# One PSUM bank for the filter layer, two for the sums, and sums last in a step, in a graph layer on one core

## The chip, the cores and the metric

The kernel runs on one core of a Trainium2 chip. The engines of the core are TensorE (PE, with its weight loads PEld), VectorE (DVE), ScalarE (ACT), GpSimd (POOL) and SyncE (SP, which issues most of the DMAs). PSUM, the memory that TensorE writes into, has eight banks of 512 f32 numbers a partition. The metric is the time of one execution in microseconds (us), the median of repeated runs.

## The reference

One layer of message passing on a graph of 12500 atoms and 412500 edges, each atom and each filter with 128 features. Each edge goes from a `src` row to a `dst` row; `dst` is sorted, `src` is not. Cut to what is computed:

```python
h = jnp.maximum(_layernorm(x), 0.0)
h = h @ W_in2f                                   # 12500 x 128
Wij = ssp(edge_attr_20 @ W_f1 + b_f1) @ W_f2 + b_f2   # filter layer, 412500 x 128
Wij = Wij * edge_weight[:, None]
x_ij = h[dst] * Wij                              # a message for each edge
agg = segment_sum(x_ij, src, 12500)              # summed by src
out = x + ssp(agg @ W_o1 + b_o1) @ W_o2 + b_o2
```

`ssp` is softplus less log 2.

## The kernel before, in words

The edges are cut into 828 **chunks** of up to 512 edges, four chunks to a **group**. For each chunk the kernel computes the hidden layer of the filter from 20 edge features (`hidden`, L819: TensorE matmuls into a tile `z`), softplus of it in two steps on ScalarE (`hidden_exp`, L828, with a running sum into `exps` that is checked at the end, and `hidden_log`, L835), the filter values (`value`, L935: four 128-column products into a bank `v`, onto a bias that ScalarE wrote there at L932), the rows of h that belong to the edges (`pick`, L944, into a bank `picked`; `picked`, L952, scales them on ScalarE into `hg`) and the message `o` = v times hg (`message`, L961, VectorE at L968 or L1107). Each message row is then written to a **slot** in a table in HBM that belongs to its source row's block of 128 atoms. `put` (L971) does that with GpSimd: one indirect DMA for each 128 rows, so four for a chunk (L977). The slot numbers come from ranks that TensorE counts in the bank `free` (`rank`, L847: matmuls at L900 and L867) and VectorE reads (`rank_end`, L871: L872).

32 of the groups (the list `SORTED`) are **permuted**: their chunks hold 424 edges and are sorted by source block on the chip beforehand, so that three quarters of the rows go to fixed places with plain DMAs and only one indirect DMA a chunk is left (L1113). `Permute` prepares such a group some 19 steps ahead; `move` (L1295) multiplies by one-hot matrices, into the same tile `z` as the filter layer, and `moved` (L1303) copies the result out on ScalarE.

The edges are also cut into seven segments, each with its own table. When a segment's table is full, `Collect` reads it back in units: `load` (a DMA into a tile `m`, five buffers), `compare` (VectorE, L1388: a one-hot matrix `to`), `add` (TensorE, L1404: the products are summed in a bank `acc`, four blocks to a bank) and `keep` (VectorE, L1427, or ScalarE, L1425, for the first segment: the bank is added to `agg`). The last segment is collected behind the last chunk, together with the output layer (`finish`, L555), which writes `out`.

The order of the work on each engine is written out by hand in `step(k)` (L1487), called once for each chunk: each engine executes its instructions in the order in which `step` names them, and waits on semaphores where it needs another's result. The step works on several chunks at once: in step k the message of chunk k, the value of k+1, the pick of k+2, the rank of k+6 and the hidden layer of k+4. A scatter of chunk k also waits until pick k+2 is done (`PACE`, L26), and a scatter that writes into one of the 16 views of a table waits for the one before it in that view.

The eight banks of before: `z` has two (both chunks of a pair), `acc` one, `v` three in turn (shared by `picked`), `free` one, and `bank` one, half of it constants and half of it room for counts. The layer norm's `xps` and `hps` (L476, L484) use the `acc` bank as well.

Of the kernel before, what the change touches and what calls it, by code (L numbers as in the profile page):

```python
# [18 lines left out]
P = 128  # L19
# [48 lines left out]
def gnn_kernel(  # L68
# [151 lines left out]
    exps = sbuf("exps", [P, ceil_div(NCH, 2)])  # L220
# [93 lines left out]
    def ranges(psum):  # L314
# [13 lines left out]
        nbad = psum.tile([P, QT, P], F32, name="nbad", tag="acc")[:1, 0, :1]  # L328
# [103 lines left out]
    def late_biases(psum):  # L432

        nc.vector.tensor_scalar(nbo1, bo1, -1.0, None, op0=ALU.mult)
        b12 = psum.tile([P, QT, P], F32, name="b12_out", tag="acc")[:, 0, :]
        nc.tensor.matmul(b12, bo1.to_broadcast([P, P]), wo2, start=True, stop=True)
        nc.vector.tensor_add(bo2, b12, bo2)
# [5 lines left out]
    def make_h(q, psum, halves=False):  # L443
# [32 lines left out]
        xps = psum.tile([P, QT, P], F32, name="xps", tag="acc")  # L476
# [7 lines left out]
        hps = psum.tile([P, QT, P], F32, name="hps", tag="acc")  # L484
# [69 lines left out]

    def finish(t0, n, sT, quad, psum, z, xo=None, bank=("v", 3)):  # L555
# [26 lines left out]
    def anyway(edge, quad, psum):  # L582
# [10 lines left out]
        with tc.For_i(0, NGA, 1) as g:  # L593
# [15 lines left out]
            for c in range(NCHUNK):  # L609
                z = psum.tile([P, 2, CH], F32, name="z")[:, 0, :]  # L610
# [43 lines left out]
        for t0 in range(0, NTILE, QT):  # L654
# [8 lines left out]
            z = psum.tile([P, 2, CH], F32, name="z_out", tag="z")[:, 0, :]  # L663
# [4 lines left out]
    with tc.tile_pool(name="edge", bufs=2) as edge, tc.tile_pool(  # L668
        name="quad", bufs=3
    ) as quad, tc.tile_pool(name="psum", bufs=1, space=PSUM) as psum, tc.tile_pool(name="state_ps", bufs=1, space=PSUM) as state_ps:  # L670
        NB = 2
# [61 lines left out]
        class Group:  # L733


            def __init__(self, g):
# [31 lines left out]
                self.out = {}  # L768

# [49 lines left out]
            def hidden(self, c):  # L819

                z = psum.tile([P, 2, CH], F32, name="z")
                for k in range(2):
                    rows = slice(32 * (c + k), 32 * (c + k) + RBF)
                    nc.tensor.matmul(z[:, k, :], wf1[rows, :], self.f[rows, :],  # L824
                                     start=True, stop=True)
                self.pair[c] = z

            def hidden_exp(self, c):  # L828
                z = self.pair[c]
                i = (self.g * NCHUNK + c) // 2  # L830
                r = quad.tile([P, 2, CH], F32, name="r", bufs=RB)
                nc.scalar.activation(r, z, AF.Exp, bias=bf1, accum_out=exps[:, i:i + 1])  # L832
                self.pair[c] = r

            def hidden_log(self, c):  # L835
                r = self.pair[c]
# [162 lines left out]
        class Permuted(Group):  # L999
# [22 lines left out]
            def hidden(self, c):  # L1022

                z = psum.tile([P, 2, CH], F32, name="z")
                ev = self.from_.ev[c // 2]
                for k in range(2):
                    for q in range(3):
                        nc.tensor.matmul(z[:, k, :], w1s[:, q, :], ev[:3 * WR, k, :],
                                         start=q == 0, stop=q == 2)
                self.pair[c] = z  # L1030
# [95 lines left out]
        class Permute:  # L1126


            def __init__(self, g):
# [30 lines left out]
            def bank(self):  # L1160
                if not self.early:
                    return room_ps
                t = psum.tile([P, QT, P], F32, name="acc_p", tag="acc")
                return t.rearrange("p c f -> p (c f)")

            def load(self):
                if self.early:
                    a0 = rows_at + 5 * NC + 8 + self.w0 // NCHUNK % 2 * (256 + 2 * QB)
                    assert a0 + 256 + 2 * QB <= NTILE * P
# [125 lines left out]
            def move(self, c):  # L1295
                if c % 2 == 0:
                    self.z = psum.tile([P, 2, CH], F32, name="z")
                parts = self.slabs.pop(c).bitcast(BF16).rearrange("p (j n h) -> p j n h", j=QT, h=2)
                for j, h in enumerate(self.hot.pop(c)):
                    nc.tensor.matmul(self.z[:, c % 2, :], parts[:, j, :, 1], h, start=j == 0,  # L1300
                                     stop=j == QT - 1)

            def moved(self, c):  # L1303
                self.ev[c // 2] = quad_room().bitcast(BF16).rearrange("p (w e) -> p w e", w=2)
                nc.scalar.activation(self.ev[c // 2], self.z, AF.Copy)
# [31 lines left out]
        class Collect:  # L1337


            def __init__(self, seg):  # L1340
# [15 lines left out]
                self.banks = [("acc", 1)]  # L1356
# [36 lines left out]
            def add(self, u):  # L1393
                b0, nb, t0, nt = self.units[u]
                m, to = self.m.pop(u), self.to.pop(u)
                for j in range(nb * nt):
                    b, t = b0 + j // nt, t0 + j % nt
                    i = b % self.size
                    if i == 0 and t == 0:
                        tag, bufs = self.banks[b // QT % len(self.banks)]  # L1400
                        self.acc[b // QT] = psum.tile([P, QT, P], F32, name="acc", tag=tag,
# [497 lines left out]
```

## Time and profile before

| what | us |
|---|---|
| median of three runs | 3897.16 (3892.02 to 3898.47) |
| the profiled execution, its own time | 3887.55 |
| its span, first to last instruction | 3885.5 |
| TensorE busy | 3319.8 |
| VectorE busy | 3054.3 |
| GpSimd busy | 2829.7 |
| ScalarE busy | 2477.1 |

The rows quoted below have these columns. In a group of instructions: line, engine, operation, `out<-in` with partitions x elements and type, xcount, then busy time in all, mean ns of one, and the idle time of the engine just before them with what ended most of it. In a row of the timeline: start, duration, engine, line, operation, count, and in brackets the idle time before it and what released it. "issue" is idle time in which the engine waited for nothing that the profile shows. In a table of stretches: busy time of each engine with its number of instructions, the granted clock of TensorE, the share of the DMA engines' time and what they moved. DMAs that SyncE issues stand as SPq.

### The profile page before, as it was taken

The page shows a single profiled execution, that of the slowest core. Times are in us where ns is not written, and L with a number is a line of the kernel's source. Part 1 is how long each engine was busy: PE and PEld are TensorE (multiplying, and loading weights), DVE is VectorE, ACT ScalarE, POOL GpSimd, SP SyncE. Part 2 cuts the span into 40 slices and gives each one's busy share as a digit, 9 for nine tenths or more (in the row PEclk, how much of TensorE's full clock was granted, in tenths as well). Part 3 has the DMA queues.
Part 4 walks back from the last instruction along what each step waited for, and adds up shares of the span by engine and source line. Part 5 has one row for each costly group of instructions (what it writes and reads, how often), then busy time and mean ns, then how long its engine had stood idle before and what let it go on. Part 6 is the DMA issues. An engine that isn't in the chain of part 4 may idle for free. (4 is left out here: it accounts for less than half of the span.)

```text
span 3885.5 us, 79865 instructions
## 1 busy us (share of the span) xinstructions
PE 3319.8 (85%) x24510; PEld 2644.5 (68%) x24560; DVE 3054.3 (79%) x8306; ACT 2477.1 (64%) x5728; POOL 2829.7 (73%) x2946
## 2 busy tenths in 40 slices
PE   6787887877778888888889989998989989898869
PEld 4555555545457677677667777777778777787767
DVE  7887878776668778887788878888877777788777
ACT  5777777867667766676667666666555555565525
POOL 5777777777777777777777777777777777777760
PEclk9888888888789999999999999999999999999999
DMA  6787767755567776688767788788988898777767
GB/s 172 220 281 246 198 185 193 201 172 149 155 197 224 214 214 191 184 245 248 197 185 198 210 260 241 217 225 264 282 232 228 227 271 237 224 226 209 194 195 192
DMA packets 669996, 835.54 MB, mean 215 GB/s; under 512 B 238252, under 2 KB 475700, under 8 KB 669560
## 3 DMA queue, kind: packets, MB, share of 16 engines
q1 hardware_dynamic: 575432, 636.64, 59.9%
q0 software_dynamic: 93696, 193.58, 15.0%
q8 instruction: 198, 3.24, 0.4%
q14 instruction: 238, 1.95, 0.2%
q10 hardware_dynamic: 432, 0.13, 0.0%
HBM read 425.40 MB, written 404.54 MB: 214 GB/s over the span
## 5 line engine op out<-in xcount | busy, mean ns | idle before, releaser
L977 POOL DMA_INDIRECT slots<-o,slot x2800 | 2702.6, 965 | 898.9 <-issue 610.9
L1404 PEld LDWEIGHTS acc<-to,m 128*128 128x128 f32 x8328 | 1056.9, 204 | 342.3 <-DVE to L1388 130.7
L1404 PE MATMUL acc<-to,m 128*128 128x128 f32 x8328 | 1142.7, 293 | 149.0 <-DVE to L1388 63.1
L939 PEld LDWEIGHTS v<-wf,r 128*128 128x128 f32 x6624 | 924.3, 208 | 140.1 <-ACT v L932 79.8
L939 PE MATMUL v<-wf,r 128*128 128x128 f32 x6624 | 960.6, 292 | 53.1 <-ACT v L932 52.9
L832 ACT ACTIVATE r<-z,bf 128x1024 f32<-128x1024 f32 x414 | 459.7, 1110 | 662.6 <-PE z L824 587.6
L957 ACT ACTIVATE hg<-picked,rcut 128x128 f32<-128x128 f32 x2800 | 791.6, 369 | 77.9 <-PE picked L948 72.3
L932 ACT ACTIVATE v<-bf 128x512 f32<-128x512 f32 x826 | 497.0, 602 | 427.7 <-DVE o L968 365.4
L1388 DVE TENSOR_TENSOR to<-count_ps,m 128x640 f32<-128x640 f16 (+4 forms) x939 | 666.2, 736 | 55.3 <-DMA m<-slots 29.0
L968 DVE TENSOR_TENSOR o<-v,hg 128x512 f32<-128x512 f32 x700 | 478.7, 684 | 108.5 <-ACT hg L957 57.0
L837 ACT ACTIVATE r<-r,half 128x1024 f32<-128x1024 f32 x414 | 470.4, 1136 | 0.0
L872 DVE TENSOR_REDUCE top<-free 128x4 f32<-128x392 f32 x700 | 388.3, 555 | 93.4 <-PE free L867 92.1
L948 PE MATMUL picked<-near,at 96*128 96x128 bf16 x2800 | 289.2, 228 | 189.7 <-DVE o L968 83.3
L824 PE MATMUL z<-f,wf 20*128 20x512 f32 x1400 | 431.2, 694 | 0.0
L841 DVE TENSOR_TENSOR inb<-count_ps,blk 128x392 f16<-128x392 f16 x700 | 388.5, 556 | 51.8 <-PE count_ps L1239 39.7
L948 PEld LDWEIGHTS <-at 96*128 96x128 bf16 x2800 | 230.0, 103 | 224.5 <-issue 193.5
L900 PE MATMUL free<-inb,rest_of 128*128 128x392 f16 x732 | 258.5, 353 | 49.1 <-DVE top L872 48.5
L966 DVE COPY o<-place 128x8 f32<-128x8 f32 x350 | 68.3, 195 | 241.4 <-DMA slots<-o,slot 195.6
L867 PE MATMUL free<-inb,after 128*128 128x392 f16 x700 | 248.3, 355 | 8.5 <-DVE used L906 6.0
L919 DVE TENSOR_SCALAR at<-rel,prow 96x512 bf16<-96x512 bf16 x700 | 252.9, 362 | 0.0
L1113 POOL DMA_INDIRECT slots<-o,slot_p x128 | 124.4, 972 | 39.0 <-issue 18.0
L1097 ACT ACTIVATE hg<-picked,scalars 128x128 f32<-128x128 f32 x512 | 144.3, 366 | 4.1 <-PE picked L1085 3.9
(228 smaller groups left out, 2735.1 us busy)
## 6 DMA issues: line engine op xcount, KB each, us to landing
m<-slots SPq DMA_DIRECT2D x458, 322.5 KB
rel<-rel_d SPq DMA_DIRECT2D x175, 384.0 KB
m<-slots SPq DMA_DIRECT2D x150, 387.0 KB
slots<-zero SPq DMA_DIRECT2D x106, 516.0 KB
slots<-o,slot POOLq DMA_INDIRECT x2800
f<-in_f_n SPq DMA_DIRECT2D x412, 80.0 KB
slots<-zero SPq DMA_DIRECT2D x122, 258.0 KB
fix<-o SPq DMA_DIRECT2D x128, 193.5 KB
```

The source lines that it names most:

```text
L824: nc.tensor.matmul(z[:, k, :], wf1[rows, :], self.f[rows, :], start=True, stop=True)
L832: nc.scalar.activation(r, z, AF.Exp, bias=bf1, accum_out=exps[:, i:i + 1])
L837: nc.scalar.activation(r, r, AF.Ln, bias=half, scale=0.5)
L841: nc.vector.tensor_tensor(inb, count_ps[:, None, :NBLK].to_broadcast([P, QT, NBLK]), self.blk[:, c * QT:(c + 1) * QT, None].to_broadcast([ ...
L932: nc.scalar.activation(v, spread(bf2, QT), AF.Copy)
L939: done = nc.tensor.matmul(v[:, i, :], r[:, i * P:(i + 1) * P], wf2, start=False, stop=True, skip_group_check=True)
L948: done = nc.tensor.matmul(ps[:, i, :], at[:, i * P:(i + 1) * P], near, start=i == 0, stop=i == QT - 1, skip_group_check=True)
L957: nc.scalar.activation(hg[:, i, :], ps[:, i, :], AF.Copy, scale=self.rcut[:, j:j + 1])
L968: nc.vector.tensor_mul(o[:, :, :P], v, hg)
L977: put = nc.gpsimd.indirect_dma_start(out=views[j % VIEWS], out_offset=bass.IndirectOffsetOnAxis(ap=self.slot[:, j:j + 1], axis=0), in_=o[: ...
L1388: nc.vector.tensor_tensor(to[:p, a:e, :], count_ps[:p, None, :].to_broadcast([p, e - a, P]), self.m[u][:p, a:e, P:].to_broadcast([p, e - a ...
L1404: nc.tensor.matmul(self.acc[b // self.size][:, i, :], m[:p, j, :P], to[:p, j, :], start=t == 0, stop=t == self.seg.read(b) - 1)
```

## The change

The banks are dealt out anew. `z` has one bank, and the filter layer's first product and its exponential go chunk by chunk instead of by pairs; the logarithm still takes a pair. The freed bank becomes a second one for sums: `acc_quad` hands out `acc0` and `acc1` in turn, and while a sum is open, the other one to everybody else. The moves of the sorting take these banks, one chunk at a time, instead of `z`. `exps` has a column for each chunk. The output layer's two `z_out` are `z` and `acc1`, no longer the halves of `z`. The order inside a step changes: the window (L919) comes first, the logarithm and then the exponential stand behind the message and the scatters, ranks come ahead of the hidden layer, which runs five chunks ahead instead of four, and the layer norm's second half, `keep` and `add` come last.

```diff
+    turns = {"last": 1, "held": None, "pool": None}
+    def acc_quad(name):
+        t = 1 - (turns["last"] if turns["held"] is None else turns["held"])
+        turns["last"] = t
+        return turns["pool"].tile([P, QT, P], F32, name=name, tag=f"acc{t}")
...
             def hidden(self, c):
-                z = psum.tile([P, 2, CH], F32, name="z")
-                for k in range(2):
-                    rows = slice(32 * (c + k), 32 * (c + k) + RBF)
-                    nc.tensor.matmul(z[:, k, :], wf1[rows, :], self.f[rows, :],
-                                     start=True, stop=True)
-                self.pair[c] = z
+                z = psum.tile([P, CH], F32, name="z")
+                rows = slice(32 * c, 32 * c + RBF)
+                nc.tensor.matmul(z, wf1[rows, :], self.f[rows, :], start=True, stop=True)
+                self.z_of[c] = z
...
                 nc.scalar.activation(r, z, AF.Exp, bias=bf1, accum_out=exps[:, i:i + 1])
...
             def move(self, c):
-                if c % 2 == 0:
-                    self.z = psum.tile([P, 2, CH], F32, name="z")
+                self.z = acc_bank("z_p")
...
-                    put(-9 + c // 2 * 2, "product", self.move, c)
-                for c in range(0, NCHUNK, 2):
-                    put(-8 + c, "moved", self.moved, c)
+                    put(-10 + c, "product", self.move, c)
+                    put(-9 + c, "moved", self.moved, c)
...
-                        self.acc[b // QT] = psum.tile([P, QT, P], F32, name="acc", tag=tag,
-                                                      bufs=bufs)
+                            home = acc_quad("acc")
+                            turns["held"] = turns["last"]
...
-        LG, LW, LR, LZ = 10, 6, 6, 4
+        LG, LW, LR, LZ = 10, 6, 6, 5
...
             statics.clear()
+            part("window", k + 3, window)
             sorting(k, "moved")
-            part("log", min(k + LZ - 2, made["exp"]), pairs(hidden_log))
-            part("exp", min(k + LZ - 1, made["hidden"]), pairs(hidden_exp))
...
+            part("log", min(k + LZ - 2, made["exp"] - (made["exp"] < NCH - 1)), pairs(hidden_log))
...
+            for c, u in units:
+                c.compare(u)
+                compared.append((c, u))
             if has(k):
                 g, c = of(k)
                 g.put(c)
-            part("window", k + 3, window)
-            for c, u in units:
-                c.compare(u)
-                compared.append((c, u))
-            for c in owed:
-                c.keep()
-            owed.clear()
+            part("exp", min(k + LZ - 1, made["hidden"]), hidden_exp)
+            sorting(k, "product")
...
-            part("hidden", k + LZ, pairs(hidden))
-            sorting(k, "product")
-            for c, u in compared:
-                c.add(u)
-            compared.clear()
...
-            sorting(k, "ready")
+            part("hidden", k + LZ, hidden)
             for c, u in units:
                 c.load(u + AHEAD)
+            for m in aside:
+                next(m, None)
+            for c in owed:
+                c.keep()
+            owed.clear()
+            for c, u in compared:
+                c.add(u)
+            compared.clear()
+            sorting(k, "ready")
...
             part("exp", 0, hidden_exp)
-            part("log", 0, hidden_log)
+            part("hidden", 1, hidden)
+            part("exp", 1, hidden_exp)
+            part("log", 1, pairs(hidden_log))
...
-            last.banks = [("acc", 1), ("v", 3)]
-            z = psum.tile([P, 2, CH], F32, name="z_out", tag="z")
+            last.banks = [("acc0", 1), ("v", 3)]
+            z = [psum.tile([P, CH], F32, name="z_out", tag=t) for t in ("z", "acc1")]
```

Three places show what stands in a row now. The first is TensorE at the program's start (`xps` and `hps` are the transpose and the product of the layer norm, `z` the hidden layer, `free` the ranks). Before:

```order
L478 MATMUL xps<-ident,xb 128x128 [waits DMAHW0_49,DVE_49,Pool_49]
L478 MATMUL xps<-ident,xb 128x128 [waits DVE_49] x3
L824 MATMUL z<-f,wf_62 128x512 [waits DMAHW7_49,DMAHW3_49]
L824 MATMUL z<-f,wf_62 128x512 [waits DMAHW4_49,DMAHW0_49]
L486 MATMUL hps<-win,xT 128x128 [waits DMAHW5_49,Activation_49]
```

And with the change, on the same engine at the same place:

```order
L478 MATMUL xps<-ident,xb 128x128 [waits DMAHW0_49,DVE_49,Pool_49]
L478 MATMUL xps<-ident,xb 128x128 [waits DVE_49] x3
L836 MATMUL z<-f,wf_62 128x512 [waits DMAHW7_49,DMAHW3_49]
L486 MATMUL hps<-win,xT 128x128 [waits DMAHW5_49,Activation_49]
L486 MATMUL hps<-win,xT 128x128 x3
L879 LDWEIGHTS after
L879 MATMUL free<-inb,after 128x392 [waits DVE_49]
L836 MATMUL z<-f,wf_62 128x512 [waits DMAHW4_49,DMAHW0_49,Activation_49]
```

One of the two hidden products has moved from ahead of `hps` to behind the first rank, and waits for ScalarE.

The second place is TensorE in an ordinary step in the last third of the program, from the last product of the pick on. Before:

```order
L948 MATMUL picked<-near,at 128x128
L824 MATMUL z<-f,wf_62 128x512 x2
L1404 MATMUL acc<-to,m 128x128 [waits DMAHW2_49,DVE_49]
L1404 MATMUL acc<-to,m 128x128 x4
L900 LDWEIGHTS rest_of
L900 MATMUL free<-inb,rest_of 128x392 [waits DVE_49]
L867 LDWEIGHTS after
L867 MATMUL free<-inb,after 128x392
L939 MATMUL v<-wf_63,r 128x128 [waits Activation_49]
```

With the change:

```order
L960 MATMUL picked<-near,at 128x128
L912 LDWEIGHTS rest_of
L912 MATMUL free<-inb,rest_of 128x392 [waits DVE_49]
L879 LDWEIGHTS after
L879 MATMUL free<-inb,after 128x392
L836 MATMUL z<-f,wf_62 128x512 [waits Activation_49]
L1417 MATMUL acc<-to,m 128x128 [waits DMAHW2_49]
L1417 MATMUL acc<-to,m 128x128 x4
L951 MATMUL v<-wf_63,r 128x128 x4
```

The ranks stand ahead of the hidden product and the sums behind it; the hidden product waits for ScalarE in each step, the sums no longer wait for VectorE.

The third place is ScalarE in the same stretch. Before, over two steps:

```order
L837 ACTIVATE r<-r,half 128x1024
L957 ACTIVATE hg<-picked,rcut 128x128 [waits DVE_49,PE_49]
L957 ACTIVATE hg<-picked,rcut 128x128 x3
L932 ACTIVATE v<-bf_68 128x512 [waits DVE_49]
L832 ACTIVATE r,exps<-z,bf_66 128x1024 [waits PE_49]
L957 ACTIVATE hg<-picked,rcut 128x128 x4
L932 ACTIVATE v<-bf_68 128x512 [waits Activation_49]
```

With the change, over two steps:

```order
L849 ACTIVATE r<-r,half 128x1024 [waits Activation_49]
L969 ACTIVATE hg<-picked,rcut 128x128 [waits DVE_49,PE_49]
L969 ACTIVATE hg<-picked,rcut 128x128 x3
L944 ACTIVATE v<-bf_68 128x512 [waits Activation_49]
L845 ACTIVATE r,exps<-z,bf_66 128x512 [waits PE_49]
L969 ACTIVATE hg<-picked,rcut 128x128 [waits DVE_49,PE_49]
L969 ACTIVATE hg<-picked,rcut 128x128 x3
L944 ACTIVATE v<-bf_68 128x512 [waits Activation_49]
L845 ACTIVATE r,exps<-z,bf_66 128x512 [waits PE_49]
```

One exponential of 1024 columns in two steps has become one of 512 columns at the end of each.

More of the change, by code (lines that the diff above doesn't have):

```diff
@@ L483, in make_h @@
         yield
-        hps = psum.tile([P, QT, P], F32, name="hps", tag="acc")
+        hps = acc_quad("hps")
         for i in range(n):
@@ L1022, in hidden @@
             def hidden(self, c):
-                z = psum.tile([P, 2, CH], F32, name="z")
+                z = psum.tile([P, CH], F32, name="z")
                 ev = self.from_.ev[c // 2]
[L1026 to L1030, printed above, removed]
+                for q in range(3):
+                    nc.tensor.matmul(z, w1s[:, q, :], ev[:3 * WR, c % 2, :],
+                                     start=q == 0, stop=q == 2)
+                self.z_of[c] = z
             def over(self, i):
@@ L1408, in add @@
                         owed.append(self)
+                        turns["held"] = None
             def ends(self, u):
@@ L1514, in step @@
                 vs[k + 1] = g.value(c, bs.pop(k + 1))
-            for m in aside:
-                next(m, None)
             if has(k + 2):
```

53 lines of the change are left out of this document (31 added, 22 removed).

## The prediction

> **What bounds the kernel now.** I read the slices of the page first, then the groups, then the timeline of GpSimd from its first scatter to its last.
>
> ```profile
> POOL 5777777777777777777777777777777777777760
> L977 POOL DMA_INDIRECT slots<-o,slot x2800 | 2702.6, 965 | 898.9 <-issue 610.9
> L1113 POOL DMA_INDIRECT slots<-o,slot_p x128 | 124.4, 972 | 39.0 <-issue 18.0
> ```
>
> TensorE is busy longest, but GpSimd's row is the flat one: the same seven tenths in every slice between the first and the last. That is what an engine looks like that does one thing at a fixed pace.
>
> ```profile
> 32.97 1.13 POOL L977 DMA_INDIRECT slots<-o,slot  x1 [29.42 <-PE picked L948]
> 34.40 0.96 POOL L977 DMA_INDIRECT slots<-o,slot  x1 [0.30 <-issue]
> 35.66 0.96 POOL L977 DMA_INDIRECT slots<-o,slot  x1 [0.30 <-issue]
> 36.92 0.96 POOL L977 DMA_INDIRECT slots<-o,slot  x1 [0.30 <-issue]
> 39.69 0.95 POOL L977 DMA_INDIRECT slots<-o,slot  x1 [1.81 <-DVE top L872]
> ...
> 3767.47 0.96 POOL L977 DMA_INDIRECT slots<-o,slot  x1 [0.30 <-issue]
> ```
>
> A scatter takes 0.96 us and 0.30 us pass before the next, which waits for nothing that is shown. Of 2800 + 128 = 2928 scatters each thus costs 1.26 us, 3689 us together. The stream runs from 32.97 to 3768.43, which is 3735.5 us; the groups give the same: 2702.6 + 898.9 + 124.4 + 39.0 less the first wait of 29.4. So the span of 3885.5 is a **start** of 33.0, a **stream** of 3735.5 and an **end** of 117.1, and at most 46 us of the stream are anything but scatters at their pace. The change adds and removes no scatter.
>
> The other engines work for this stream and wait for it:
>
> ```profile
> DVE o L966 <- DMA slots<-o,slot: 195.6, 94, 5.4
> DVE o L1104 <- DMA slots<-o,slot: 83.0, 20, 8.1
> ACT v L932 <- DVE o L968: 365.4, 168, 8.6
> ```
>
> VectorE stands 279 us waiting for a message buffer that a scatter has not yet given back, and ScalarE waits behind it. Within the stream, then, a faster step buys nothing, and a slower one costs nothing until these waits are used up. The time can move at the start, at the end, or in the 46 us.
>
> **The change, part by part.** The exponential goes from 414 instructions of 1024 columns to 828 of 512.
>
> ```profile
> L832 ACT ACTIVATE r<-z,bf 128x1024 f32<-128x1024 f32 x414 | 459.7, 1110 | 662.6 <-PE z L824 587.6
> L832 ACT ACTIVATION_READ_ACCUMULATOR r<-z,bf 128x1 f32 x414 | 79.9, 193 | 0.0
> L837 ACT ACTIVATE r<-r,half 128x1024 f32<-128x1024 f32 x414 | 470.4, 1136 | 0.0
> L957 ACT ACTIVATE hg<-picked,rcut 128x128 f32<-128x128 f32 x2800 | 791.6, 369 | 77.9 <-PE picked L948 72.3
> L932 ACT ACTIVATE v<-bf 128x512 f32<-128x512 f32 x826 | 497.0, 602 | 427.7 <-DVE o L968 365.4
> L490 ACT ACTIVATE left<-hps 128x512 f32<-128x512 f32 (+1 forms) x25 | 15.3, 613 | 13.0 <-PE hps L486 13.0
> ```
>
> No row shows an exponential of 512; the nearest, a copy of 512 out of PSUM, takes 613 ns. With a read of the accumulator each that makes 828 x 0.806 = 667 against 540 us: 128 us more for ScalarE, 0.15 us a chunk. The sorting's copies, halved too, add some 14 us in the same way. Now the hidden product of chunk k+5 waits in each step for the exponential of k+4, since `z` is one bank. Queued behind it on TensorE are the sums, the next values and the next pick, and for these GpSimd waits. ScalarE's round is 4 x 0.369 + 0.602 + 0.806 + half of 1.136 = 3.5 us; a chunk of four scatters takes 5.05. The cover is 1.6 us a chunk, so I put both at **nothing** in the stream. If the cover were gone, the whole exponential of 0.81 us would stand in a step; that is a rival below.
>
> The second bank of sums removes a wait of TensorE:
>
> ```profile
> PE acc L1404 <- DVE agg L1427: 56.6, 46, 4.2
> PEld acc L1404 <- DVE agg L1427: 85.2, 58, 5.0
> ```
>
> The two overlap, so 57 to 85 us of TensorE. In the stream they are worth nothing, for the reason above; where scatters have ended, they count. Ranks ahead of the hidden product, sums behind it, `keep` behind the ranks: these only reorder work that the stream covers, again except at the two ends. Seven of the 128 moves take a bank whose sum has just ended and then wait for its `keep`; that is under 3 us each of TensorE, and covered by the same waits.
>
> **The start.** The layer norm's product stands behind two hidden products, of which one moves away.
>
> ```profile
> 8.80 2.08 PE L824 MATMUL z<-f,wf 20*128 20x512 f32 x4
> 10.80 2.08 PE L486 MATMUL hps<-win,xT 128*128 128x128 f32 x8
> 14.21 0.69 DVE L494 TENSOR_TENSOR left<-left,hb 128x512 f32<-128x512 f32 x1 [0.46 <-ACT hb L492]
> 32.60 2.08 PE L824 MATMUL z<-f,wf 20*128 20x512 f32 x4
> 34.61 0.51 PE L900 MATMUL free<-inb,rest_of 128*128 128x392 f16 x1
> 35.48 0.57 DVE L872 TENSOR_REDUCE top<-free 128x4 f32<-128x392 f32 x1 [4.54 <-PE free L867]
> ```
>
> One product is 1.04 us here. On the way to the stored h, VectorE had waited only 0.46 us for this chain and is busy before that, so the first scatter comes **0.5 us** earlier. The second chunk's first scatter, at 39.69, waited 1.81 us where 0.30 is the rule; its message was late because VectorE had waited 4.54 us for ranks that stood behind the hidden pair of 32.60. With ranks first, that pair's 2.08 us leave the chain and the 1.5 us of excess can go. Bounds: 0 and 2.0 us. I take **2.0**, because the row removed (2.08) is longer than the excess.
>
> **The waits in the stream.** Besides the one at 39.69, sixteen waits before a scatter exceed 0.35 us; the first and the last:
>
> ```profile
> 252.88 0.95 POOL L977 DMA_INDIRECT slots<-o,slot  x1 [2.00 <-DVE top L872]
> 2633.61 0.96 POOL L977 DMA_INDIRECT slots<-o,slot  x1 [0.94 <-DVE inb L841]
> ```
>
> Together they hold 14.4 us above the rule. Most stand at the first scatter behind the four of a permuted group, and the engines named differ each time. In the code this scatter writes into the view that the fourth scatter before it wrote, so I read them as waits for that landing. The change leaves that order alone and only shifts when other DMAs are in flight: **0**, with bounds of -14.4 (gone) and +14.4 (doubled).
>
> **The end.** After the last message the steps hold only `compare`, `keep` and `add`.
>
> ```profile
> 3740.00:3760.00 20.00, 13.86 (x112) 12.72 (x110) 13.99 (x22) 0.00 (x0) 15.12 (x17) 1.00 0.94 260
> ...
> 3748.22 2.05 PE L1404 MATMUL acc<-to,m 128*128 128x128 f32 x16 [0.78 <-DVE agg L1427]
> 3749.31 0.96 DVE L1388 TENSOR_TENSOR to<-count_ps,m 128x768 f32<-128x768 f16 x1 [1.14 <-DMA m<-slots]
> 3766.53 4.57 PE L1404 MATMUL acc<-to,m 128*128 128x128 f32 x24 [3.50 <-DVE agg L1427]
> 3771.88 2.94 PE L1404 MATMUL acc<-to,m 128*128 128x128 f32 x24 [0.78 <-DVE agg L1427]
> 3772.83 30.07 SPq L1366 DMA_DIRECT2D m<-slots  x17
> 3777.14 0.58 DVE L1754 TENSOR_REDUCE most<-exps 128x1 f32<-128x414 f32 x1
> 3782.77 2.47 DVE L1388 TENSOR_TENSOR to<-count_ps,m 128x768 f32<-128x768 f16 x4
> ```
>
> TensorE waits 0.8 us or more for `keep` in each round of 2.8 us. Without it a round is still held by the loads of `m`: the DMA engines are at 0.94 and VectorE waits for `m` as well. What is sure are the last sums, whose bursts no longer stand behind a `keep`: 0.6 us at 3766.53 (from the compare's end to `keep`'s), then 0.78 and 0.78, and some 1.5 us over the ten rounds before. That makes 3.7. `keep` before 3777.14, the check of `exps`, the x loads' biases and the first `compare` of the last segment at 3782.77 follow in a row on VectorE, so they come earlier by as much. The floor is the load issued at 3772.83, which waits for the last scatters; a load lands in some 4 us, so the first compare can be no earlier than 3777: a bound of 5.8 us, the other being 0. The check reads 828 columns instead of 414: 0.4 us more. I take **-3.1** for the end. From there on TensorE is busy throughout (20.0 of 20 us in each stretch from 3800) with the same instructions, and the two `z_out` alternate as the halves did.
>
> The 24 sums at 3766.53 took 4.57 us behind a pause of 3.50, the 24 at 3771.88 behind a short one 2.94. The Trainium skill, in "TensorE: Matmul & The Clock Gate", section "What's actually happening", says that TensorE's clock falls to half after an idle window of about 3.4 us; these two rows agree. By that rule the end would gain up to 1.6 us more, since the pause shrinks to 2.9; by the row alone it doesn't. I leave it out of the sum.
>
> **Sum.** -2.0 - 3.1 + 0 = -5.1 us on the profiled execution of 3887.55 (span 3885.5): 3882.4. The runs' median, 3897.16, is 9.6 us above that execution; on that scale the forecast is **3892.0**. Two thousandths, 7.8 us, is about what a measurement of this kernel can tell from no change, so this would read as no change.
>
> **The rivals.** *Slower: the first twenty chunks can't carry the waits for the exponential.*
>
> ```profile
> 43.44 0.39 PE L948 MATMUL picked<-near,at 96*128 96x128 bf16 x4
> 44.73 0.96 POOL L977 DMA_INDIRECT slots<-o,slot  x1 [0.30 <-issue]
> 50.00:60.00 10.00, 6.23 (x43) 4.18 (x43) 9.51 (x35) 9.53 (x24) 7.87 (x8) 1.00 0.43 135
> ```
>
> Here the lead is thin: the pick that releases the scatter of 44.73 ends 0.6 us before it is due, and between 50 and 60 us VectorE and ScalarE are both over 95% busy. If each step grew by the whole 0.81 us, eighteen chunks would cost 14.5 us and the start's gain is gone: 3897.2 + 14.5 - 3.1 = 3908.6. It decides from a step that grows by more than the 0.6 us; the added ScalarE work alone (0.15) doesn't reach that. Against it: in these steps VectorE is the longer one, and its work stays the same. Chance 0.17.
>
> *Faster: the landings come in time.* All 14.4 us of waits go, and the end gains its 5.8: 3892.0 - 14.4 - 2.7 = 3875. For it: sums and loads spread differently. Against: the DMA bytes are the same. Chance 0.13. The opposite, landings later by as much, 3906: 0.07.
>
> *Nothing arrives.* The end stays with its loads and the start with VectorE: 3897. Chance 0.13. The forecast, between 3888 and 3895, keeps 0.5.
>
> **Range and chances.** 3878 to 3908: the forecast, the case of nothing, most of the slower one, and half of the landings. Faster by over 0.2% (under 3889.4): 0.13 and a third of the forecast's half, 0.29. Slower (over 3904.9): 0.16. Within: 0.55.
>
> **What would show it.** Right: GpSimd's seven tenths stay flat, scatters keep 965 ns and 0.30 us, the stream lasts 3725 to 3740 us; the wait at the second chunk is gone; no sum waits for `keep`; the first `compare` of the last segment begins 2 to 6 us sooner behind the last scatter. ScalarE's busy time rises by about 140 us and the time doesn't follow. Wrong: waits of GpSimd between chunks 2 and 20, or behind each permuted group, with pick or message as the late one; then a step has become longer than I think.

## The result, and the profile after

| | before | changed kernel |
|---|---|---|
| median, four runs each | 3895.8 us | 3923.19 us (3917.67 to 3927.77) |
| ratio | 1 | 1.0071, 95% interval 1.0059 to 1.0084 |
| profiled execution, its own time | 3887.55 us | 3927.77 us |
| span | 3885.5 us | 3926.1 us |
| start, to the first scatter | 33.0 us | 34.1 us |
| stream, first scatter to the end of the last | 3735.5 us | 3783.9 us |
| end, behind the last scatter | 117.1 us | 108.1 us |

The change costs 27 us, 0.7%. The forecast was 3892, its range ended at 3908. The spans of the two profiled executions lie 40.6 us apart, since that of before was 8 us quicker than its median and the other 5 us slower than its own; the terms below add up to the 40.6.

From the page of the changed kernel: its busy times, GpSimd's slices, and two of its groups:

```profile
PE 3699.3 (94%) x24537; PEld 2638.2 (67%) x24560; DVE 3063.3 (78%) x8306; ACT 2646.5 (67%) x6620; POOL 2826.8 (72%) x2946
POOL 4777777677777777777777776777777777777760
L989 POOL DMA_INDIRECT slots<-o,slot x2800 | 2699.8, 964 | 942.4 <-issue 619.8
L845 ACT ACTIVATE r<-z,bf 128x512 f32<-128x512 f32 x828 | 556.8, 672 | 53.2 <-PE z L836 48.8
```

Scatters still take 0.96 us, and GpSimd's row is nearly flat, with a six in two places ahead of the end. The line that had changed most is TensorE's: it is busy for 3699 us where it had been 3320, though the change neither adds nor removes a product. The group of the hidden products, first of before, then of the changed kernel, shows where it is:

```profile
L824 PE MATMUL z<-f,wf 20*128 20x512 f32 x1400 | 431.2, 694 | 0.0
```

```profile
L836 PE MATMUL z<-f,wf 20*128 20x512 f32 x1400 | 851.7, 690 | 21.7 <-ACT r L845 21.1
```

The count is the same and so is the mean of one, 0.69 us, but the busy time has doubled. (TensorE as a whole rose by 379 us and not by these 420, because other groups took less, the sums above all: 1107.1 us for 1142.7.) In before 1400 x 0.694 is 972 us; a group that is busy for 431 us must have had its records lying beside each other. Rows of the timelines of TensorE, before and after, show it directly:

```profile
2403.17 1.13 PE L824 MATMUL z<-f,wf 20*128 20x512 f32 x4
```

```profile
2400.39 1.12 PE L836 MATMUL z<-f,wf 20*128 20x512 f32 x2
2401.44 1.38 PE L1417 MATMUL acc<-to,m 128*128 128x128 f32 x10
2402.66 1.06 PE L951 MATMUL v<-wf,r 128*128 128x128 f32 x8
2403.55 0.39 PE L960 MATMUL picked<-near,at 96*128 96x128 bf16 x4
...
2404.37 1.12 PE L836 MATMUL z<-f,wf 20*128 20x512 f32 x2
2405.42 2.50 PE L1417 MATMUL acc<-to,m 128*128 128x128 f32 x20
2407.75 1.06 PE L951 MATMUL v<-wf,r 128*128 128x128 f32 x8
2408.65 0.39 PE L960 MATMUL picked<-near,at 96*128 96x128 bf16 x4
```

Two products (four records) took 1.13 us, and now one (two records) takes 1.12. The features of chunk c lie in partitions from 32 c on, so the two products of a pair use different rows of TensorE. The Trainium skill, in "TensorE: Matmul & The Clock Gate", section "Part 3: Packing small matmuls — row/col tiling", says that small matmuls can be put on different tiles of the array, in steps of 32 rows, and then run at the same time; these rows agree. The single products of the changed kernel have 128-row matmuls on both sides and run alone. By the busy times of the groups a product cost 0.62 us before (431.2 / 700) and costs 1.22 now (851.7 / 700): 700 x 0.60 us = 420 us more for TensorE.

Where TensorE has no room for it, picks come late. The stretch from 2000 to 2700 us, before and after (behind the length stand TensorE, its weight loads, VectorE, ScalarE and GpSimd):

```profile
2000.00:2700.00 700.00, 634.03 (x5065) 524.20 (x5078) 590.71 (x1550) 457.63 (x1064) 526.14 (x548) 0.96 0.80 225
```

```profile
2000.00:2700.00 700.00, 677.38 (x4819) 502.31 (x4822) 558.33 (x1487) 461.72 (x1165) 499.70 (x521) 0.96 0.74 209
```

Before, TensorE had 700 - 634 = 66 us of room here. GpSimd's 548 instructions are 32 scatters of permuted groups and 516 others, which is 129 ordinary chunks, and 129 x 0.60 us = 77 us more don't fit. In the second row 27 scatters fewer were done in the same time. GpSimd's timeline of the changed kernel shows what they waited for, in the first chunks and in this stretch:

```profile
47.82 0.96 POOL L989 DMA_INDIRECT slots<-o,slot  x1 [2.45 <-PE free L912]
54.83 0.96 POOL L989 DMA_INDIRECT slots<-o,slot  x1 [2.27 <-PE free L912]
2404.22 0.96 POOL L1124 DMA_INDIRECT slots<-o,slot_p  x1 [2.26 <-PE count_ps L1248]
2409.32 0.96 POOL L989 DMA_INDIRECT slots<-o,slot  x1 [4.14 <-PE picked L960]
```

The scatter at 2409.32 waited for the pick at 2408.65 in the rows of TensorE above; from 2404.37 on a product, the sums, a value and this pick stand there without a gap. ScalarE tells the same in the list of waits (total, times, longest), before and after:

```profile
ACT hg L957 <- PE picked L948: 72.3, 64, 4.3
```

```profile
ACT hg L969 <- PE picked L960: 489.2, 338, 5.1
```

Each wait of a scatter above the usual 0.30 us can be put into one of three classes by the trace's records of DMA landings. It is a **landing** if the scatter starts a fixed time behind the landing of the scatter that wrote the same view before it (0.77 or 0.78 us in every kernel here that has such waits); otherwise it is **early** if it lies in the first 140 us, and **late** if it comes later. In us above the 0.30:

| kernel | landing | late | early |
|---|---|---|---|
| before | 14.2 | 0.2 | 1.5 |
| changed | 14.7 | 46.6 | 6.1 |

So 40.6 is: start +1.1, early +4.6, late +46.4, landings +0.5, the scatters' own time -3.0 (2824.0 us for 2827.0), end -9.0. Of the 27 late waits of the changed kernel, 26 end 0.28 us behind the end of a pick on TensorE, and these hold 46.4 of the 46.6 us: late means a late pick. 38.6 of the 46.6 lie between 2000 and 2706 us, and 7.8 between 744 and 781, where the granted clock was low (0.62 from 700 to 785). 33.0 of them stand at the last scatters of a permuted group or in the group behind it. A permuted group has one scatter a chunk, so GpSimd passes through its four chunks in about 5 us where it otherwise needs 20, and asks for the next picks that much sooner; I read the place of the waits so, and tested it no further.

The end became shorter by 9 us, more than forecast. First the last `keep` of before; then, in the changed kernel, the last scatter, the last `keep`, the loads and the first compare of the last segment:

```profile
3776.80 0.42 DVE L1427 TENSOR_TENSOR agg<-agg,acc 128x256 f32<-128x256 f32 x1 [0.65 <-PE acc L1404]
```

```profile
3816.93 0.69 DVE L1441 TENSOR_TENSOR agg<-agg,acc 128x512 f32<-128x512 f32 x1 [1.00 <-PE acc L1417]
3817.05 0.96 POOL L989 DMA_INDIRECT slots<-o,slot  x1 [0.31 <-issue]
...
3818.14 0.41 DVE L1441 TENSOR_TENSOR agg<-agg,acc 128x256 f32<-128x256 f32 x1
3818.47 1.01 DVE L1770 TENSOR_REDUCE most<-exps 128x1 f32<-128x828 f32 x1
...
3821.56 23.61 SPq L1375 DMA_DIRECT2D m<-slots  x17
...
3824.97 1.29 DVE L1397 TENSOR_TENSOR to<-count_ps,m 128x768 f32<-128x768 f16 x2 [0.37 <-DMA m<-slots]
```

Before, the last `keep` began 8.4 us behind the end of the last scatter and the first compare 14.3; now it is 0.1 and 7.0. The sums of the sixth segment are no longer left over.

### The profile page after: what moved, and what is told of

Same layout as the page of the kernel before. It is cut to its first block, busy times and chain, and to the rows that moved or that the text cites. A ratio compares the mean times of both kernels' runs of the same rounds, so it can differ in the third digit from the quotient of the medians.

```text
span 3926.1 us, 80357 instructions
## 1 busy us (share of the span) xinstructions
PE 3699.3 (94%) x24537; PEld 2638.2 (67%) x24560; DVE 3063.3 (78%) x8306; ACT 2646.5 (67%) x6620; POOL 2826.8 (72%) x2946
## 5 line engine op out<-in xcount | busy, mean ns | idle before, releaser
L1417 PEld LDWEIGHTS acc<-to,m 128*128 128x128 f32 x8328 | 1010.4, 197 | 399.4 <-issue 231.6
L1417 PE MATMUL acc<-to,m 128*128 128x128 f32 x8328 | 1107.1, 287 | 20.4 <-DVE to L1397 13.3
L951 PEld LDWEIGHTS v<-wf,r 128*128 128x128 f32 x6624 | 883.7, 207 | 184.9 <-issue 178.0
L951 PE MATMUL v<-wf,r 128*128 128x128 f32 x6624 | 972.5, 294 | 0.0
L836 PE MATMUL z<-f,wf 20*128 20x512 f32 x1400 | 851.7, 690 | 21.7 <-ACT r L845 21.1
L845 ACT ACTIVATE r<-z,bf 128x512 f32<-128x512 f32 x828 | 556.8, 672 | 53.2 <-PE z L836 48.8
L836 PEld LDWEIGHTS z<-f,wf 20*128 20x128 f32 x1400 | 219.1, 195 | 271.5 <-issue 199.2
L1314 ACT ACTIVATE xo<-z_p 128x512 bf16<-128x512 f32 x128 | 76.0, 594 | 133.8 <-PE z_p L1308 133.0
```

Of the source, the lines that this page charges most:

```text
L836: nc.tensor.matmul(z, wf1[rows, :], self.f[rows, :], start=True, stop=True)
L951: done = nc.tensor.matmul(v[:, i, :], r[:, i * P:(i + 1) * P], wf2, start=False, stop=True, skip_group_check=True)
L1417: nc.tensor.matmul(self.acc[b // self.size][:, i, :], m[:p, j, :P], to[:p, j, :], start=t == 0, stop=t == self.seg.read(b) - 1)
```

## The experiments

Two theories stood against each other. **A**: what was lost is the side-by-side running of the two products of a pair. **B**: the waits for ScalarE in the single bank, or the new order of the step, make steps longer. Ratios are to the kernel before in the same set.

**One strip.** The kernel before, with the features of both chunks of a pair in the same 32 partitions. The input array is laid out for it; banks, order and number of instructions stay.

```diff
-                self.f = kept["f"][:, g % NB, :]
+                self.f = kept["f"]
+                self.odd = (g % NB, g == NG - 1 and NG % NB == 1)
...
+                b, alone = self.odd
...
-                    rows = slice(32 * (c + k), 32 * (c + k) + RBF)
-                    nc.tensor.matmul(z[:, k, :], wf1[rows, :], self.f[rows, :],
+                    j = c + k if alone else 2 * b + c // 2
+                    rows = slice(32 * j, 32 * j + RBF)
+                    nc.tensor.matmul(z[:, k, :], wf1[rows, :],
+                                     self.f[rows, 0 if alone else k, :],
...
+        "f_n": one_group(np.ascontiguousarray(
...
```

> The kernel before with one edit: the features of both chunks of a pair lie in the same 32 partitions, so that their two hidden products use the same rows of TensorE; banks, order and instructions stay. Theory A (products on different rows ran side by side, 1.13 us for the pair; one behind the other they take 2.26): TensorE's busy time rises by 350 x 1.13 = 395 us to about 3700, the stream of scatters waits where TensorE has no room, 2000 to 2700 us above all, and the time comes to 3910 to 3935. Theory B (the slowdown of the change comes from its waits for ScalarE or from the new order): the pair's time does not matter, 3890 to 3902.

Measured: 3932.18 us, ratio 1.0091 (1.0074 to 1.0108). A row of TensorE's timeline in this kernel, and its group:

```profile
2759.98 1.98 PE L827 MATMUL z<-f,wf 20*128 20x512 f32 x4
```

```profile
L827 PE MATMUL z<-f,wf 20*128 20x512 f32 x1400 | 735.1, 647 | 0.0
```

A pair takes 1.98 us (less than the 2.26 expected), TensorE's busy time rises by 266 us to 3585.4 (395 were expected), and the stream lasts 3773.6 us with 15.9 us of late waits, 8.6 early and 30.8 of landings. Moving 20 rows by 32 partitions costs more than the whole change, so A holds in direction, and the time lies in its range. But only the 15.7 us of late and 7.1 of early waits more are of the kind that A is about; 16.6 are landings that came later, as they do in the run with the new order below.

**Products by themselves.** A kernel that has only these matmuls, 40 rounds of each kind, and reads by ScalarE behind each kind.

> A kernel of its own that computes only matmuls, none of the layer: 40 times each, two products of 20 x 512 f32 on rows 0 and 32, and both on row 0, alone and with two ranks of 128 rows behind them; then the two products on rows 0 and 32 with a rank between them. Theory A (products on different rows run side by side where they stand next to each other): a pair takes 1.13 us on two strips and 2.26 on one; with two ranks between pairs about 1.6 together, 2.8 on one strip, and 2.8 apart. Theory B (the records' modelled ends only make it look so): the same time in all three.

Three stretches of it, each within one kind: both on one strip with two ranks behind them; on two strips, likewise; on two strips with a rank between them. The granted clock (0.50) is the same in all.

```profile
351.00:538.00 187.00, 186.93 (x240) 51.58 (x240) 0.00 (x0) 0.51 (x1) 0.00 (x0) 0.50 0.00 0
229.90:349.60 119.70, 119.66 (x240) 25.59 (x239) 0.00 (x0) 0.60 (x1) 0.00 (x0) 0.50 0.00 0
539.90:742.60 202.70, 202.68 (x240) 47.47 (x238) 0.00 (x0) 0.00 (x0) 0.00 (x0) 0.50 0.00 0
```

A round takes 187.0 / 40 = 4.68 us on one strip, 119.7 / 40 = 2.99 on two, and 202.7 / 40 = 5.07 when a 128-row matmul stands between. Pairs with nothing behind them take 1.66 us on two strips (66.3 us from 27.2 on, granted clock 0.53) and 3.39 on one (135.7 us from 94.2 on, 0.50). The stretches end where ScalarE's reads could start, so these times do not rest on the modelled ends of matmuls, and theory B of this run falls. The three are 1.7 to 1.9 times those expected (1.6, 2.8 and 2.8), in their relation about as A has it.

**Half the product.** The changed kernel with TensorE's extra time taken away: only the first 256 columns of an ordinary chunk's hidden product are computed, and the exponential reads these twice. Half of the hidden layer is left out. Banks, waits, order and ScalarE's work stay.

```diff
-                nc.tensor.matmul(z, wf1[rows, :], self.f[rows, :], start=True, stop=True)
-                self.z_of[c] = z
+                w = CH // 2
+                nc.tensor.matmul(z[:, :w], wf1[rows, :], self.f[rows, :w], start=True, stop=True)
+                self.z_of[c] = z[:, None, :w].to_broadcast([P, 2, w])
...
+                if len(z.shape) == 3:
+                    r = r.rearrange("p (a b) -> p a b", a=2)
```

> The changed kernel, in which the hidden product of an ordinary chunk computes only its first 256 columns and the exponential reads these twice; half of the filter's hidden layer is left out. TensorE's time for a product falls from 1.12 to 0.56 us, what it took before in a pair; ScalarE's work, banks, waits and order stay. Theory A (TensorE's lost time makes the picks late): TensorE's busy time falls by 390 us to about 3300, the late picks (some 50 of 67 us) go, and the time falls by 30 to 45 us to 3878 to 3893. Theory B (the waits for the single bank, or the order, make the step longer): the picks stay late, 3910 to 3925.

In that set of runs the kernel before itself took 4897 us, and this one 4909.78 (ratio 1.0026). In its profile scatters wait for 1033 us above the 0.30, where they wait for 67 in the changed kernel, so it tells nothing of a stream that goes at GpSimd's pace. Once more, in a set where before takes 3895 us:

> The same kernel as half_hidden (the changed kernel, half of the hidden layer's columns left out), since the kernel before took 4897 us in that set, a quarter more than in all others. Theory A (TensorE's lost time makes the picks late): 3878 to 3893 where the kernel before takes 3897, TensorE busy about 3300 us, few late picks. Theory B (the single bank's waits or the order): 3910 to 3925.

Measured: 3889.44 us, ratio 0.9990 (0.9980 to 1.0001). Busy times and a group of its page, then the stretch from 2000 on:

```profile
PE 3461.6 (89%) x24549; PEld 2687.9 (69%) x24560; DVE 3052.3 (79%) x8306; ACT 2638.5 (68%) x6620; POOL 2828.3 (73%) x2946
L837 PE MATMUL z<-f,wf 20*128 20x256 f32 x1400 | 534.1, 463 | 35.2 <-ACT r L848 32.5
```

```profile
2000.00:2700.00 700.00, 655.79 (x5044) 527.07 (x5046) 585.19 (x1539) 484.45 (x1225) 518.87 (x540) 0.97 0.78 221
```

Half a product takes 0.76 us (534.1 / 700) and not 0.56, so TensorE only fell to 3461.6. That is enough: from 2000 to 2700 GpSimd does 540 instructions where it did 521, late waits are 8.6 us instead of 46.6, early ones 2.0, and landings stay at 16.8. With ScalarE's work as in the changed kernel (2638.5), with the single bank and the new order, the time is that of before. A shorter product could also give the single bank back sooner, but TensorE waits no less for the exponential in front of these products: 32.5 us, where it was 21.1 in the changed kernel. So the 34 us between this and the changed kernel go with TensorE's time. B has at most the 8.6 us that stay, 8.4 of them behind picks; the run with the new order alone, below, has as much.

**The landings.** In before, and in the changed kernel, the four scatters of a permuted group write into other views, so that ten scatters lie between two on one view and not four.

```diff
-                    out=self.seg.views[c * QT % VIEWS],
+                    out=self.seg.views[6 + c],
```

> The kernel before with one edit: the four scatters of a permuted group write into views 6 to 9 instead of 0, 4, 8 and 12, so that ten scatters lie between two on one view, not four. Theory A (the waits of a first scatter behind a permuted group are waits for the landing of the fourth scatter before it): of 15.9 us above the rule in the stream, at most 3 stay, and the time falls by some 12 us to 3884. Theory B (they are something else): 3893 to 3899, with the same waits.

Before with this edit: 3881.52 us, ratio 0.9953 (0.9937 to 0.9970). Landings 0, late 2.1, early 4.0, stream 3724.9; the end grew to 123.8 us. The prediction's reading of these waits is shown. Where before waited 0.64 us (at 1697.79, as a wait for VectorE by the trace), the first scatter behind the permuted group is now

```profile
1692.91 0.95 POOL L977 DMA_INDIRECT slots<-o,slot  x1 [0.30 <-PE picked L948]
```

> The changed kernel with the views of permuted groups at 6 to 9. In its profile 67 us of the stream are waits of scatters, about 15 of them behind a landing on the same view and the rest behind a late pick. Theory A (TensorE's lost time stays, only the landings go): the late picks stay with 40 us or more, the time falls by 10 to 18 us to 3905 to 3913. Theory B (all the added waits are landings): the stream falls to 3725, and the time to 3870 to 3880.

The changed kernel with it: 3911.4 us, ratio 1.0034 (1.0022 to 1.0047). Landings 0, late 40.0, early 6.3. It gains 12 us, as A has it, and keeps the late picks.

**The order alone.** Before, with its banks and pairs, and the step written in the changed kernel's order.

```diff
+            part("window", k + 3, window)
             sorting(k, "moved")
-            part("log", min(k + LZ - 2, made["exp"]), pairs(hidden_log))
-            part("exp", min(k + LZ - 1, made["hidden"]), pairs(hidden_exp))
...
                 tops.append(r)
+            part("hidden", k + LZ, pairs(hidden))
+            sorting(k, "product")
...
+            for c in owed:
+                c.keep()
+            owed.clear()
+            for c, u in compared:
+                c.add(u)
+            compared.clear()
```

> The kernel before with its own banks and pairs, and the step written in the order of the changed kernel (window first, logarithm and exponential behind the message, ranks ahead of the hidden products, keep and sums last). Theory A (the slowdown is TensorE time lost by single products, the order costs nothing): the stream keeps its 3735 us within 10, 3886 to 3898. Theory B (the order of the step makes steps longer): 3908 to 3925, with waits for picks in the stream. If the order gives the shorter end, the end is 108 to 112 us.

Measured: 3911.55 us, ratio 1.0036 (1.0021 to 1.0050), so B's time; the end is 120.0 us, so the order does not shorten it. The stream is 20.8 us longer, with 29.8 us of landings, 8.4 late and 2.1 early. One of the landings, at the place shown above for the other views:

```profile
1706.96 0.96 POOL L977 DMA_INDIRECT slots<-o,slot  x1 [2.42 <-PE picked L948]
```

To tell whether the landings carry it, the other views were to be added:

> The kernel before with the step in the new order, and the views of permuted groups at 6 to 9 (only the order and the views differ from before). Theory A (what the order cost were landings that came later, 30 of its 40 us of waits): the time falls to 3880 to 3888, some 7 us of late picks stay. Theory B (the order makes steps longer): 3900 to 3910, with late picks in place of the landings.

The kernel of that run does not have the other views; it is the kernel of the order alone again, and says only that its time repeats: 3911.78 us, landings 30.6. With the views, in the set in which before took 4897 us, it took 4904.63 (ratio 1.0027):

> The kernel before with the step in the new order and with the views of permuted groups at 6 to 9 (the run order_views had been given the file without the views, and repeated order_alone). Theory A (what the order costs are landings on the same view): the waits behind landings, about 30 us of 40 to 45, go, and the time falls to 3880 to 3888. Theory B (the order makes steps longer, and late picks take the landings' place): 3900 to 3912.

And once more, in the other set:

> The same kernel as order_6to9 (before, the new order of the step, views 6 to 9), for the same reason. Theory A (what the order costs are landings on the same view): 3880 to 3888. Theory B (the order makes steps longer, late picks take the landings' place): 3900 to 3912.

3884.33 us, ratio 0.9976 (0.9964 to 0.9987); landings 0, late 11.8, early 2.1, and the late waits all end 0.28 us behind a pick. So B is not all wrong. In the profile of the order alone 15.6 us more are landings than in before and 8.2 more are late; and with the landings gone, the order still costs about 9 us against before with the same views (0.9976 against 0.9953, with intervals that just overlap). Why the landings come later in that order was not found out; in the changed kernel itself they do not (14.7).

**The second bank.** The changed kernel, with sums in one bank; then before, with sums in `acc` and in the free bank of `z` in turn once the filter layer is done; then this with the other views.

```diff
-        t = 1 - (turns["last"] if turns["held"] is None else turns["held"])
-        turns["last"] = t
+        t = 0 if name == "acc" else 1
...
-                            turns["held"] = turns["last"]
```

> The changed kernel with one edit: sums use one bank, so they wait for keep again; the second bank is left to the moves and the layer norm. Theory A (the second bank shortens the end): the end behind the last scatter goes back from 108 to 114 to 117 us, and the stream waits more where TensorE is full, 3928 to 3945. Theory B (the end is shorter because of the order of the step): 3920 to 3927, end 108 to 110.

3923.55 us (ratio 1.0073, 1.0056 to 1.0090), the same as with two banks. Neither theory has it: the time is B's, the end is A's, and the stream moved against A. In the profile the end grows to 115.8 us, with the last keep at 3809.45, 8.2 us behind the last scatter,

```profile
3809.45 0.42 DVE L1439 TENSOR_TENSOR agg<-agg,acc 128x256 f32<-128x256 f32 x1 [0.65 <-PE acc L1415]
```

and the stream shrinks to 3767.1 us, with 27.8 us of late waits for 46.6. I read it so that sums which do not wait for `keep` take TensorE from picks where it is full; that is argued from one profile each, not shown. The two profiled executions also lie 9 us apart where the medians are equal.

```diff
+                        if self.banks == [("acc", 1)] and turns["free"]:
+                            turns["z"] = not turns["z"]
+                            if turns["z"]:
+                                tag, bufs = "z", 1
...
+            turns["free"] = made["exp"] >= NCH - 2
             sorting(k, "product")
```

> The kernel before; once the last exponential of the filter layer is issued, sums alternate between the acc bank and the bank of z that has come free. Theory A (the second bank shortens the end, since sums of the sixth segment are no longer left over behind the last scatter): the last keep comes within 2 us of the last scatter where it took 8.4, the end falls from 117 to 108 to 111, the time to 3886 to 3891. Theory B (the loads bound these sums): last keep at 6 us or more, 3893 to 3898.

3887.19 us, ratio 0.9974 (0.9965 to 0.9984). The last keep comes 0.5 us behind the last scatter, the end is 109.4 us. At the end, where scatters no longer hide it, the second bank is worth 8 us.

> Both edits on the kernel before: views 6 to 9, and the second bank for sums at the end. With the views alone the last keep came 15.1 us behind the last scatter. If the bank shortens the end (A): 3866 to 3873. If the loads bound it (B): 3878 to 3884.

**3870.3 us, ratio 0.9931 (0.9914 to 0.9947)**: a version that beats both kernels. It keeps the pairs of before. Its only waits in the stream are 3.1 us in the first 140, and the sums end with the stream, whose last scatter ends at 3759.13:

```profile
3758.99 0.69 DVE L1435 TENSOR_TENSOR agg<-agg,z_acc 128x512 f32<-128x512 f32 x1 [0.50 <-PE z_acc L1412]
3760.19 0.41 DVE L1435 TENSOR_TENSOR agg<-agg,acc 128x256 f32<-128x256 f32 x1
3766.77 1.29 DVE L1388 TENSOR_TENSOR to<-count_ps,m 128x768 f32<-128x768 f16 x2 [0.55 <-DMA m<-slots]
```

## Why the prediction was wrong

**The bound was right.** The stream at 0.96 + 0.30 us a scatter sets the time, and other engines count where their slack, the time that they spend waiting, ends. What was wrong is whose slack ended.

**The step that failed** is the price of the hidden products. The prediction costed the exponential's 128 us on ScalarE and gave the product that moved with it no cost at all: "One product is 1.04 us here", half of a row of four records in 2.08. That halving is false; in the changed kernel one product at the same place takes as long as the two:

```profile
8.73 2.07 PE L836 MATMUL z<-f,wf 20*128 20x512 f32 x2
```

The page held the contradiction, 1400 records with a mean of 694 ns in 431 us of busy time; the prediction never showed this group. The records of the two products lay side by side, so one product alone takes as long as two, and the term for these products is +420 us of TensorE, not 0. That in the stream a slower step "costs nothing until these waits are used up" was true, and was not checked for TensorE: the 66 us of room from 2000 to 2700 were used up, and 46.6 us of late picks came of it. The sign that the prediction named for being wrong did show, waits behind permuted groups with the pick as the late one. None of the rivals had this cause; the slower one had the right place in part (the first chunks), but another mechanism and 14.5 us, where 4.6 were lost there.

**ScalarE** was right in substance: +128 +14 us were forecast and 169 came (an exponential took 672 ns, not the 613 of a copy), and they stayed hidden, as half the product shows.

**The start** was forecast at -2.0 us. It came +1.1 late with 4.6 us of early waits, by the same cause: the single product ahead of the layer norm takes the 2 us that the pair took (the row above), and the other products come on top. With half the product the first scatter came at 32.50, 0.5 us earlier as forecast, but early waits were 2.0: 0.4 at the second chunk, and 1.6 now at the third. Of the 1.5 us that the forecast took there, none was gained.

**The landings** were read rightly, and their 0 held: 14.2 and 14.7 us. (The prediction counts sixteen waits; the trace has seventeen, with the 14.4 us that it gives.)

**The end** had the right mechanism and was too small: -3.1 forecast, -9.0 measured. The bound of 5.8 took the issue of the loads at 4.4 us and four more for the landing as fixed; now the loads are issued 3.5 us behind the last scatter, and the first compare comes at 7.0. Of the 9.0, 7.4 are there, and 1.6 behind it. The clock, which the prediction left out of its sum, fits as a part of the 7.4: before, the granted clock was 0.50 from 3766.8 to 3770.2, under the sums that begin at 3766.53; in the changed kernel it is 1.00 from 3784.9 to 3822.4, through all of the last sums. (By its own terms the prediction's sum for the end is -3.7 + 0.4 = -3.3 and not -3.1.)

Put together without the failing step, the forecast's ratio is 3892.0 / 3897.16 = 0.9987, and the changed kernel with half the product measured 0.9990; that the two agree is partly luck, since single terms missed in both directions.

## What to carry to other kernels

Before matmuls are moved apart, multiply the count of their group by the mean of one and compare it with the busy time: where busy is much less (431 us for 972 here), they run side by side, and one alone may cost as much as the pair. An engine that is off the critical path needs its room checked by stretches, at the new cost, not on the average. A second bank for sums pays where sums are the last to end, and there a bank that has just come free will do (-7.7 us at the end here).

## What the runs showed of the hardware

- Two products of 20 x 512 f32 on different strips of 32 rows take 1.13 us together, one alone 1.12, two on one strip 1.98. With a 128-row matmul between them a round took 5.07 us, next to each other 2.99 (granted clock 0.50).
- Half the columns do not halve such a product: by the busy times of the groups, 0.76 us for 256 columns (534.1 us for 700) and 1.22 for 512 (851.7 for 700).
- A scatter that is held by its view starts a fixed time behind the landing of the one before it there (0.77 or 0.78 us in every kernel here that has such waits). The trace names some engine as the releaser; the landing records name the cause.
- A scatter that is held by a late pick starts 0.28 us behind the pick's end (26 of 27 late waits of the changed kernel).
